# Graph layer with a sorted scatter: the load order at the start, the seam between two stages, and the pace of the sort's steps

## The chip, the cores and the metric

The kernel runs on one core of a Trainium2 chip. The time is device microseconds from start to end of one execution. PE is TensorE (matmuls; PEld its weight loads), DVE is VectorE, ACT is ScalarE, POOL is GpSimd and SP is SyncE, which here only issues transfers. Each engine works through its own list of instructions in order.

## The reference

```python
def reference(x, src, dst, edge_weight, L0_gnn_weight, L0_ffn_W, L0_ffn_b):
    # x (8192, 512); src, dst, edge_weight (131072,)
    h = layernorm(x) @ L0_gnn_weight.T
    x = x + segment_sum(edge_weight[:, None] * h[dst], src, 8192)
    x = x + ffn(layernorm(x))
    return x
```

`ffn` takes a few columns of a normalized row, turns groups of 16 into two small numbers, sends them through seven layers of width 160, and adds one-hot codes of the two rounded results to 32 columns, where a mask holds. It returns the normalized rows with these codes added. The edges come in the order of `dst`, while the sum runs over `src`: the kernel sorts them itself by blocks of 128 values of `src`.

## The kernel before

The nodes are 64 blocks of 128 rows. The edges of a block are cut into tiles of 128: 6 tiles a block in a first part (384 tiles) and 11 in a second (704). For a tile, POOL gathers 128 rows of h from HBM with an indirect DMA (`rows_for`, L546), DVE makes a matrix with the edge's weight in the column of its row (`hot_for`, L559, a "one-hot", seven buffers of four tiles ahead), and PE multiplies the two and sums over the block's tiles (`blocks_of`, L841, two matmul passes a tile). Each buffer of four tiles also has one small matmul (L837). Six buffers of gathered rows exist (pool `gp`), so gathers can run at most 24 tiles ahead.

The work is in three stages, whose instructions are written out by hand in one order for PE, DVE, ACT and SP (`manual_schedule`).

1. **h** (`project`, L469 to L525). For 64 blocks: load x in pairs (L476, SP), statistics on DVE (`scale`, L484 to L488), normalization on ACT (L490), transposition by PE (`turn`, L499) and a copy by ACT (L501), the product by PE (L518), a copy by ACT (L520), the store to `h_rows` (L524, L522, SP). Between the blocks, the sort of the first part is dealt out.
2. **The first part's 384 tiles** (`begin`, L845). Sums are added to x (L851) and stored. Between the tiles, the sort of the second part is dealt out.
3. **The second part's 704 tiles** (`evenly`, L872). The sums give the final x; `ffn` works on units of eight blocks between the tiles.

The sort (`order`, L456) is a generator of steps. It has chunks of edges, 7 in the first part and 9 in the second (`chunk`, L248): DVE compares blocks (L254), PE sums over rows (L262), DVE sums over columns (L267) and masks (L271), PE makes ranks (L277), DVE makes places (L281 to L304, with casts by ACT, L295), and 512 matmul passes in groups put edges into their places (L321, after L313). Then `squeeze` (L329) closes the gaps: a scan (L338), and for ten bits a shift by masks on DVE (L394, L401, L408) with a copy on ACT (L398); at the end PE transposes the result (L446) and ACT writes the three arrays that say which row to gather, which row to add to, and with which weight (L448).

Each step ends with `yield tiles, blocks`: how many tiles of the first part (in stage 2), or blocks of h (in stage 1), are to pass before the next step. In stage 1 the loop adds up the second number in `due`; in stage 2 the first:

```python
            while t >= due:
                due += next(second, (NB * FT,))[0]
            if t == late_at:
                for _ in second:
                    pass
```

`late_at` is tile 355; what is left of the second sort is issued there at once, since the gathers of the second part need its result. In the first part a step works on whole rows (`fine` is 0), in the second on pieces of about 520 columns with one step each.

At the start, SP issues the loads of src, dst and the weights (L226 to L228) ahead of x (L476), ACT issues the load of the layer's weights (L156), and DVE prepares the edges (L233 to L241) ahead of the first statistics of x. After the last block of h, ten copies on ACT spread the weights of `ffn` (`spread_weights`, L213).

Of the kernel before, what the change touches and what calls it, by code (L numbers as in the profile page):

```python
# [13 lines left out]
OP = mybir.AluOpType  # L14
# [20 lines left out]
def tile_gnn_ffn(  # L35
# [51 lines left out]
    SHARE, WIDTH = 0.5, 640  # L87
# [68 lines left out]
    nc.scalar.dma_start(gw, gnn_wT.rearrange("(k p) e -> p k e", p=P))  # L156
# [12 lines left out]
    def rstd_of(pool, var_ap, n, name):  # L169
        r = pool.tile([P, n], F32, name=name)  # L170
        nc.scalar.activation(r, var_ap, AF.Sqrt, bias=eps)  # L171
        nc.vector.reciprocal(r, r)
        return r

# [45 lines left out]

    with tc.tile_pool(name="ld", bufs=1) as ld:
# [10 lines left out]

        nc.vector.tensor_scalar(low, src_i, 7, None, op0=OP.logical_shift_right)  # L233
        nc.vector.tensor_copy(blk, by_chunk(low))

# [12 lines left out]
    def chunk(ck, ps_c, q, col, fine):  # L248
# [3 lines left out]
        for cs in cut(GC, 2, fine):  # L252
            n = cs.stop - cs.start
            nc.vector.tensor_tensor(  # L254
                hot[:, cs], each.rearrange("p (o b) g -> p o b g", o=1).to_broadcast([P, n, NB, GQ]),
                blk[:, q, cs].rearrange("p c (o g) -> p c o g", o=1).to_broadcast([P, n, NB, GQ]),
                OP.is_equal)
            yield 1, 1 - fine
# [14 lines left out]
        yield 0, 2  # L273
# [35 lines left out]
        yield from prepare(0)  # L309
        yield from prepare(SUB)  # L310
        p_c = ps_c.tile([P, GQ, 2, HALF], F32, name="p_c")
        yield 0, 2
# [16 lines left out]
    def squeeze(part, sq, ps_q, fine):  # L329
# [57 lines left out]
        for bit in range(LOW, LOW + BITS):  # L387
# [16 lines left out]
            yield 0, SHARE  # L404
# [6 lines left out]
            yield 0, SHARE  # L411
# [56 lines left out]

    def project():  # L469

        pairs, parts = {}, {}

        def load(b0):
            if b0 < NB:
                t = gp.tile([P, GS, D], F32, name="g")
                nc.sync.dma_start(t[:, 0:2], rows_of(x, b0, 2))  # L476
                pairs[b0] = t

        def scale(b0):
            t = pairs[b0]  # L480
            mv = mp.tile([P, 2, 2], F32, name="mv_h", bufs=2)
            for j in range(2):
                st = mp.tile([P, 6], F32, name="st_h", bufs=2)
                nc.vector.bn_stats(st, t[:, j])  # L484
                nc.vector.bn_aggr(mv[:, j, :], st)
            rstd = rstd_of(mp, mv[:, :, 1], 2, "rstd_h")
            nmr = mp.tile([P, 2], F32, name="nmr_h", bufs=2)
            nc.vector.scalar_tensor_tensor(nmr, mv[:, :, 0], -1.0, rstd, op0=OP.mult, op1=OP.mult)  # L488
            for j in range(2):
                nc.scalar.activation(t[:, 2 + j], t[:, j], AF.Identity, bias=nmr[:, j : j + 1],  # L490
                                     scale=rstd[:, j : j + 1])

        def turn(b):
            t = pairs[b - b % 2]
            if b % 2 == 0:
                parts[b] = gp.tile([P, GS, D], F32, name="g")
            p_t = ps_g.tile([P, D], F32, name="p_g")
            for k in range(KD):
                nc.tensor.transpose(p_t[:, k * P : (k + 1) * P],  # L499
                                    t[:, 2 + b % 2, k * P : (k + 1) * P], ident)  # L500
            nc.scalar.copy(parts[b - b % 2][:, b % 2], p_t)  # L501

        for b0 in (0, 2, 4):
            load(b0)
        for b0 in (0, 2):
            scale(b0)
        turn(0)
        for b in range(NB):
            if b % 2 == 0 and b + 4 < NB:
                scale(b + 4)  # L510
            if b + 1 < NB:
                turn(b + 1)
            if b % 2 == 1:
                load(b + 5)
            t = parts[b - b % 2]
            p_h = ps_g.tile([P, D], F32, name="p_g")
            for k in range(KD):
                nc.tensor.matmul(p_h, t[:, b % 2, k * P : (k + 1) * P], gw[:, k, :],  # L518
                                 start=(k == 0), stop=(k == KD - 1))
            nc.scalar.copy(t[:, 2 + b % 2], p_h)  # L520
            if b >= NB - 2:
                nc.sync.dma_start(rows_of(h_rows, b, 1), t[:, 2 + b % 2 : 3 + b % 2])  # L522
            elif b % 2:
                nc.sync.dma_start(rows_of(h_rows, b - 1, 2), t[:, 2:4])  # L524
            yield  # L525
# [36 lines left out]
    man_ctx = ExitStack()  # L562
    man_ctx.enter_context(tc.manual_schedule(engines={PE, DVE, ACT, SP}))
    first, second, heads = order(0), order(1), project()
# [6 lines left out]
    LEAD = 2  # L571
    due, early = LEAD, 0
    for b, _ in enumerate(heads):
        while first and due <= b + 1:
# [3 lines left out]
            else:  # L578
                due += step[1]
        if first is None:  # L580
# [5 lines left out]
    assert first is None  # L586
    for t in range(early, AHEAD * GS):
        hot_for(t)
    spread_weights()
# [255 lines left out]
    def begin():  # L845
# [11 lines left out]
        for b, k, p_g in blocks_of(0):  # L857
# [5 lines left out]
            if k == TILES[0] - 1:  # L863
                last = (b, p_g)
            while t >= due:
# [250 lines left out]
```

## Time and profile before

| | |
|---|---|
| median of 13 runs | 2143.88 us (2127.63 to 2154.27) |
| the profiled execution | 2144.66 us; span of its instructions 2142.7 us |
| granted TensorE clock, mean | 0.903 |
| PE busy | 1763.1 us, 82% |
| DVE busy | 990.9 us, 46% |
| ACT busy | 388.5 us, 18% |
| POOL busy | 1123.0 us, 52%, of it gathers 1100.0 (1088 of 1011 ns) |
| DMA | 391.37 MB, 183 GB/s |
| chain that ended last | PE 61%, another queue 14%, DVE 13%, "issue" 7% |

The span is what lies between the first and the last instruction. The page of a profile gives busy time by engine, the span in 40 slices, the chain of work that ended last, and groups of instructions by line. A line of the timeline has the start in us, the duration, the engine, the line of the kernel, the operation, the tile written and those read, the shape, and how many instructions were put together; in brackets is the idle time of the engine before it, and what ended it. "issue" means that the profile shows nothing that the engine waited for. A table of stretches has one row for each stretch: its length, the busy time of each engine with a count, the granted clock, the share of time that the DMA engines were busy, and GB/s.

### The profile page before, as it was taken

The page shows a single profiled execution, that of the slowest core. Times are in us where ns is not written, and L with a number is a line of the kernel's source. Part 1 is how long each engine was busy: PE and PEld are TensorE (multiplying, and loading weights), DVE is VectorE, ACT ScalarE, POOL GpSimd, SP SyncE. Part 2 cuts the span into 40 slices and gives each one's busy share as a digit, 9 for nine tenths or more (in the row PEclk, how much of TensorE's full clock was granted, in tenths as well). Part 3 has the DMA queues.
Part 4 walks back from the last instruction along what each step waited for, and adds up shares of the span by engine and source line. Part 5 has one row for each costly group of instructions (what it writes and reads, how often), then busy time and mean ns, then how long its engine had stood idle before and what let it go on. Part 6 is the DMA issues. An engine that isn't in the chain of part 4 may idle for free.

```text
span 2142.7 us, 24058 instructions
## 1 busy us (share of the span) xinstructions
PE 1763.1 (82%) x9273; PEld 850.7 (40%) x9288; DVE 990.9 (46%) x2520; ACT 388.5 (18%) x520; POOL 1123.0 (52%) x1138
## 2 busy tenths in 40 slices
PE   6999977769889988893878598696978969787977
PEld 3655543334444444441322243342433324243444
DVE  5666577335555456489323235233342434234322
ACT  3555544301111111111000010100101001010111
POOL 4000000366666667668566666566666666656550
PEclk9999998879998999897899899797989979888986
DMA  4222322466676677676596657576676856757551
GB/s 149 91 88 88 110 79 79 143 210 208 202 239 206 188 232 216 195 222 197 181 308 179 189 166 262 167 247 196 177 258 180 265 173 207 227 163 242 182 151 42
DMA packets 140923, 391.37 MB, mean 183 GB/s; under 512 B 20352, under 2 KB 21376, under 8 KB 140800
## 3 DMA queue, kind: packets, MB, share of 16 engines
q0 software_dynamic: 87952, 286.45, 44.3%
q1 hardware_dynamic: 52320, 102.25, 14.0%
q8 instruction: 76, 1.25, 0.2%
q10 hardware_dynamic: 528, 1.05, 0.1%
q14 instruction: 47, 0.39, 0.1%
HBM read 339.33 MB, written 50.33 MB: 182 GB/s over the span
## 4 chain that ended last, share of the span: by engine, by line
PE 61%; another core or an unknown queue 14%; DVE 13%; issue 7%; ACT 3%; POOL 2%; DMA 0%; ACTq 0%; DVEq 0%; POOLq 0%
PE p_g L841 33%; PE p_g L518 8%; PE p_c L321 7%; DVE hot L559 3%; PE p_a L637 2%; PE p_a L639 2%; POOL g L546 2%; ACT blocks L295 1%; PE p_rank L277 1%; DVE w L408 1%; PE p_base L262 1%; PE p_g L499 1%; DVE word L408 1%; DVE word L401 1%
## 5 line engine op out<-in xcount | busy, mean ns | idle before, releaser
L546 POOL DMA_INDIRECT g<-h_rows,at_dst x1088 | 1100.0, 1011 | 954.3 <-issue 686.4
L841 PE MATMUL p_g<-g,hot 128*128 128x512 f32 x2176 | 1102.4, 641 | 39.6 <-issue 38.0
L841 PEld LDWEIGHTS p_g<-g,hot 128*128 128x128 f32 x2176 | 407.4, 200 | 437.1 <-issue 426.5
L559 DVE TENSOR_SCALAR hot<-lanes,at_row,at_w 128x128 f32<-128x128 f32 x1088 | 325.9, 355 | 183.7 <-remote 95.7
L518 PE MATMUL p_g<-xg,g 128*128 128x512 f32 x512 | 241.9, 617 | 32.3 <-ACT g L501 32.3
L321 PE MATMUL p_c<-put,blocks 128*64 128x40 f32 x4096 | 164.3, 240 | 57.8 <-issue 47.0
L321 PEld LDWEIGHTS p_c<-put,blocks 128*64 128x64 f32 x4096 | 148.8, 149 | 105.2 <-issue 103.7
L295 ACT CAST blocks<-hot 128x1024 f32<-128x1024 bf16 x64 | 130.7, 2081 | 307.7 <-issue 238.6
L518 PEld LDWEIGHTS p_g<-xg,g 128*128 128x128 f32 x512 | 95.9, 197 | 135.6 <-issue 98.2
L611 DVE TENSOR_SCALAR hb<-p_b,b_b 128x128 f32<-128x128 f32 (+1 forms) x54 | 18.1, 335 | 224.2 <-PE p_b L631 124.3
L304 DVE TENSOR_TENSOR put<-at,val_a 128x640 f32<-128x640 bf16 x64 | 52.7, 824 | 131.9 <-remote 100.0
L837 PEld LDWEIGHTS <-hot 128*1 128x1 bf16 x272 | 21.6, 79 | 228.4 <-issue 201.1
L267 DVE TENSOR_TENSOR cum<-cum,hot 128x512 bf16<-128x512 bf16 x112 | 47.6, 425 | 111.4 <-issue 66.1
L892 DVE TENSOR_TENSOR xu<-xu,p_g 128x512 f32<-128x512 f32 x64 | 43.7, 682 | 94.8 <-remote 64.5
L837 PE MATMUL p_j<-g,hot 128*1 128x4 bf16 x272 | 45.7, 168 | 45.6 <-DMA g<-h_rows,at_dst 28.5
L171 ACT ACTIVATE rstd_f<-mv_f,eps 128x8 f32<-128x8 f32 (+1 forms) x9 | 2.7, 301 | 438.7 <-issue 185.4
L614 ACT ACTIVATE ha<-p_a,b_a 128x512 f32<-128x512 f32 (+1 forms) x54 | 34.6, 640 | 235.0 <-PE p_a L639 95.9
L851 DVE TENSOR_TENSOR xg<-xg,p_g 128x512 f32<-128x512 f32 x64 | 43.6, 681 | 65.8 <-PE p_g L841 45.0
L731 ACT COPY back<-p_v 128x256 f32<-128x256 f32 (+1 forms) x9 | 3.3, 371 | 344.4 <-PE p_v L729 258.2
L639 PEld LDWEIGHTS p_a<-hb,w_z 128*128 128x128 f32 x360 | 52.8, 211 | 19.0 <-issue 17.9
L725 DVE COPY v<-p_v 128x128 f32<-128x128 f32 (+1 forms) x9 | 2.5, 277 | 120.9 <-remote 120.2
L729 PE MATMUL p_v<-ident,pick 128*128 128x128 f32 (+1 forms) x18 | 5.8, 422 | 63.7 <-DVE v L725 63.7
(179 smaller groups left out, 1241.6 us busy)
## 6 DMA issues: line engine op xcount, KB each, us to landing
g<-h_rows,at_dst POOLq DMA_INDIRECT x1088
g<-in_x_dram SPq DMA_DIRECT2D x32, 512.0 KB
xg<-in_x_dram SPq DMA_DIRECT2D x16, 1024.0 KB
x_rows<-xg SPq DMA_DIRECT2D x32, 512.0 KB
xu<-x_rows SPq DMA_DIRECT2D x16, 1024.0 KB
h_rows<-g SPq DMA_DIRECT2D x31, 512.0 KB
out_dram<-xu SPq DMA_DIRECT2D x7, 2048.0 KB
xg<-in_gnn_wT_dram ACTq DMA_DIRECT2D x1, 1024.0 KB
```

The source lines that it names most:

```text
L267: nc.vector.tensor_tensor(cum[:, c], cum[:, c - 1], hot[:, c - 1], OP.add)
L295: nc.scalar.copy(blocks, hot[:, c0 : c0 + SUB].rearrange("p c b g -> p c g b"))
L304: nc.vector.tensor_tensor(put[:, :, :, i, :], at[:, cs], v.to_broadcast([P, n, 2, HALF]), OP.mult)
L321: nc.tensor.matmul(p_c[h * NB : (h + 1) * NB, g], blocks[:, c, g, :], put[:, k, h], start=False, stop=last)
L518: nc.tensor.matmul(p_h, t[:, b % 2, k * P : (k + 1) * P], gw[:, k, :], start=(k == 0), stop=(k == KD - 1))
L546: nc.gpsimd.indirect_dma_start(out=g[:, k, :], out_offset=None, in_=h_rows, in_offset=bass.IndirectOffsetOnAxis(ap=at_dst[part][:, i : i + ...
L559: nc.vector.tensor_scalar(hots[n][:, k, :], lanes, at_row[part][:, i : i + 1], at_w[part][:, i : i + 1], op0=OP.is_equal, op1=OP.mult)
L639: nc.tensor.matmul(p_a[:, g, :], w_z[:, i, g, :], last_hb, start=False, stop=((g + 1) * T % 512 == 0 or g == NG - 1))
L837: nc.tensor.matmul(p_j[:, part, :], hot[:, GS - 1, :].bitcast(BF16)[:, 1:2], g.rearrange("p k d -> p (k d)").bitcast(BF16).rearrange("p (k ...
L841: nc.tensor.matmul(p_g, hot[:, i, :], g[:, i, :], start=(k == 0), stop=(k == TILES[part] - 1))
L851: nc.vector.tensor_add(xg[:, b % G, :], xg[:, b % G, :], p_g)
L892: nc.vector.tensor_add(xj, xj, p_g)
```

## The change

Five things are changed.

- At the start, ACT loads its function table, then issues the load of x's first pair, then that of the layer's weights. `project` becomes a generator whose first steps are dealt among the edge operations: the statistics of the first pair stand ahead of all edge operations, its scaling and transposition behind the first two of them, the rest behind.
- Paces in blocks of h: within a chunk two blocks before the ranks become 1.5; two before the places become one before and one after the second `prepare`; each half of a bit takes 0.7 blocks (`TURN`), not 0.5. In the second part the first comparison no longer counts 0 for all four pieces: the last counts 1.
- After the first part's sort has ended, up to 25 steps of the second part's first chunk (`BEGUN`) are dealt among the last blocks of h; all steps up to the 41st are issued behind the last block, ahead of the first tile.
- Paces in tiles: a step of a chunk still takes 1.0 tiles, one of `squeeze` 0.85 (`PACE`).
- `spread_weights` moves from behind h to tile 96 of stage 2.

Lines are numbered anew in the changed kernel: L262 becomes L342, L277 L357, L321 L402, L353 L434, L446 L527, L499 L213, L501 L215, L518 L238, L520 L240, L546 L570, L559 L583, L837 L866, L841 L870, L851 L880.

```diff
-    SHARE, WIDTH = 0.5, 640
+    SHARE, TURN, WIDTH, PACE = 0.5, 0.7, 640, (1.0, 0.85)
...
-    nc.scalar.dma_start(gw, gnn_wT.rearrange("(k p) e -> p k e", p=P))
...
+        load(0, nc.scalar)
+        nc.scalar.dma_start(gw, gnn_wT.rearrange("(k p) e -> p k e", p=P))
+        yield
+        mv, rstd = weigh(0)
+        yield
+        scale(0, mv, rstd)
+        turn(0)
+        yield
+        load(2)
+        load(4)
+        scale(2, *weigh(2))
...
+    nc.scalar.activation(over[:, 0:1], eps, AF.Sqrt)
+    heads = project()
+    next(heads)
...
+        next(heads)
         nc.vector.tensor_scalar(low, src_i, 7, None, op0=OP.logical_shift_right)
         nc.vector.tensor_copy(blk, by_chunk(low))
+        next(heads)
...
-            yield 1, 1 - fine
+            yield 1, cs.stop // GC
...
-        yield 0, 2
+        yield 0, 1.5
...
         yield from prepare(0)
+        yield 0, 1
         yield from prepare(SUB)
...
-        yield 0, 2
+        yield 0, 1
...
-            yield 0, SHARE
+            yield 0, TURN
...
-            yield 0, SHARE
+            yield 0, TURN
...
-                yield from chunk(ck, ps_c, q, col, fine)
+                for tiles, blocks in chunk(ck, ps_c, q, col, fine):
+                    yield tiles * PACE[0], blocks
...
-            yield from squeeze(part, sq, ps_q, fine)
+            for tiles, blocks in squeeze(part, sq, ps_q, fine):
+                yield tiles * PACE[1], blocks
...
-    LEAD = 2
-    due, early = LEAD, 0
+    LEAD, BEGUN = 2, 25
+    due, early, begun = LEAD, 0, 0
...
+        while first is None and begun < BEGUN and due <= b + 1:
+            due += next(second)[1]
+            begun += 1
...
+    for n in range(BEGUN + 16):
+        if n >= begun:
+            next(second)
...
-    spread_weights()
...
+            if t == NBUF[0]:
+                spread_weights()
             while t >= due:
```

`weigh` is the first half of the old `scale` (statistics and square root), `scale` the second.

More of the change, by code (lines that the diff above doesn't have):

```diff
@@ L173, in rstd_of, with project, load, weigh @@
         return r
+    def project():
+        pairs, parts = {}, {}
+        def load(b0, engine=nc.sync):
+            if b0 < NB:
+                t = gp.tile([P, GS, D], F32, name="g")
+                engine.dma_start(t[:, 0:2], rows_of(x, b0, 2))
+                pairs[b0] = t
+        def weigh(b0):
+            t = pairs[b0]
+            mv = mp.tile([P, 2, 2], F32, name="mv_h", bufs=2)
+            for j in range(2):
+                st = mp.tile([P, 6], F32, name="st_h", bufs=2)
+                nc.vector.bn_stats(st, t[:, j])
+                nc.vector.bn_aggr(mv[:, j, :], st)
+            rstd = mp.tile([P, 2], F32, name="rstd_h", bufs=2)
+            nc.scalar.activation(rstd, mv[:, :, 1], AF.Sqrt, bias=eps)
+            return mv, rstd
+        def scale(b0, mv, rstd):
+            t = pairs[b0]
+            nc.vector.reciprocal(rstd, rstd)
+            nmr = mp.tile([P, 2], F32, name="nmr_h", bufs=2)
+            nc.vector.scalar_tensor_tensor(nmr, mv[:, :, 0], -1.0, rstd, op0=OP.mult, op1=OP.mult)
+            for j in range(2):
+                nc.scalar.activation(t[:, 2 + j], t[:, j], AF.Identity, bias=nmr[:, j : j + 1],
+                                     scale=rstd[:, j : j + 1])
+        def turn(b):
+            t = pairs[b - b % 2]
+            if b % 2 == 0:
+                parts[b] = gp.tile([P, GS, D], F32, name="g")
+            p_t = ps_g.tile([P, D], F32, name="p_g")
+            for k in range(KD):
+                nc.tensor.transpose(p_t[:, k * P : (k + 1) * P],
+                                    t[:, 2 + b % 2, k * P : (k + 1) * P], ident)
+            nc.scalar.copy(parts[b - b % 2][:, b % 2], p_t)
+        load(0, nc.scalar)
[9 more added lines that the diff above has]
+        scale(2, *weigh(2))
+        for b in range(NB):
+            if b % 2 == 0 and b + 4 < NB:
+                scale(b + 4, *weigh(b + 4))
+            if b + 1 < NB:
+                turn(b + 1)
+            if b % 2 == 1:
+                load(b + 5)
+            t = parts[b - b % 2]
+            p_h = ps_g.tile([P, D], F32, name="p_g")
+            for k in range(KD):
+                nc.tensor.matmul(p_h, t[:, b % 2, k * P : (k + 1) * P], gw[:, k, :],
+                                 start=(k == 0), stop=(k == KD - 1))
+            nc.scalar.copy(t[:, 2 + b % 2], p_h)
+            if b >= NB - 2:
+                nc.sync.dma_start(rows_of(h_rows, b, 1), t[:, 2 + b % 2 : 3 + b % 2])
+            elif b % 2:
+                nc.sync.dma_start(rows_of(h_rows, b - 1, 2), t[:, 2:4])
+            yield
@@ L219, in spread_weights @@
             nc.scalar.copy(w_z[GB * g : GB * g + 3, 0, g, :], w_in[GB * g : GB * g + 3, 0, 0:P])
+    man_ctx = ExitStack()
+    man_ctx.enter_context(tc.manual_schedule(engines={PE, DVE, ACT, SP}))
+    nc.scalar.activation(over[:, 0:1], eps, AF.Sqrt)
+    heads = project()
+    next(heads)
     with tc.tile_pool(name="ld", bufs=1) as ld:
@@ L465, in order @@
                 tc.tile_pool(name="ps_q", bufs=2, space=PSUM) as ps_q:
-            yield from squeeze(part, sq, ps_q, fine)
[L469 to L525, printed above, removed]
@@ L560, in hot_for @@
                                 at_w[part][:, i : i + 1], op0=OP.is_equal, op1=OP.mult)
-    man_ctx = ExitStack()
-    man_ctx.enter_context(tc.manual_schedule(engines={PE, DVE, ACT, SP}))
-    first, second, heads = order(0), order(1), project()
+    first, second = order(0), order(1)
     def load_x(b0):
```

## The prediction

> **What bounds the kernel now.** I first read the page's 40 slices and then the table of stages (busy time of each engine per stretch), because the three stages have different limits. The stage of h, up to 401 us, is TensorE's. In the first part's blocks (412 to about 1057 us) TensorE shares with the sort of the second part. In the second part's blocks the gathers set the pace. Two places stand out. The first is a stop around 1000 us:
>
> ```profile
> 980.00:1000.00 20.00, 9.81 (x20) 3.62 (x18) 19.89 (x37) 4.50 (x3) 16.65 (x12) 0.89 0.64 204
> 1000.00:1020.00 20.00, 0.00 (x0) 0.00 (x0) 19.79 (x32) 4.14 (x4) 15.73 (x15) 0.50 0.63 182
> 1040.00:1060.00 20.00, 20.00 (x49) 8.15 (x48) 6.14 (x18) 0.00 (x0) 15.20 (x16) 1.00 0.76 235
> ```
>
> The columns are the stretch, then PE, PEld, DVE, ACT and POOL busy with counts, the granted clock, and DMA. PE is at 0 while DVE is full. The timeline of PE names the releaser:
>
> ```profile
> 990.11 3.70 PE L841 MATMUL p_g<-g,hot 128*128 128x512 f32 x8
> 1023.56 1.54 PE L446 MATMUL p_f<-ident,dst_f 128*128 128x128 f32 x6 [29.75 <-DVE dst_f L431]
> ```
>
> Counting L841's pairs in that timeline, 356 of the first part's 384 tiles are done there: at tile 355 (`late_at`) all sort steps that are left are issued at once, with TensorE's transposes of the result (L446) ahead of tile 356. So PE waits for DVE to drain the sort. The second place is the seam between h and the gathers:
>
> ```profile
> 404.82 1.01 POOL L546 DMA_INDIRECT g<-h_rows,at_dst  x1 [378.46 <-issue]
> 412.52 0.17 PE L837 MATMUL p_j<-g,hot 128*1 128x4 bf16 x1 [11.48 <-DMA g<-h_rows,at_dst]
> 412.62 6.69 PE L841 MATMUL p_g<-g,hot 128*128 128x512 f32 x8
> ```
>
> PE is idle 11.5 us for the first gathered rows, and the first eight matmuls then take 6.69 us where later rows have 3.70.
>
> The price of a gather comes next, from the busy time of L546 alone in stretches of the trace (stretch, POOL busy, clock, DMA):
>
> ```profile
> 945.00:967.00 22.00, 18.06 (x13) 1.00 0.81 250
> 967.00:990.00 23.00, 19.32 (x13) 0.85 0.78 241
> 1156.00:1180.00 24.00, 18.20 (x20) 0.93 0.67 194
> ```
>
> Undisturbed, one is issued every 1.25 us (1.2 here, with the two at the edges). While DVE is full with the bits of the sort it is every 1.73 us (45 us for 26). A tile's two matmuls take 0.93 us, so wherever the sort's bits run, the gathers are the limit.
>
> **The change, part by part.** I follow the start of the gather with number 380 (from 0), at 1034.83 us in the profiled execution, the first after the stop. From there on 708 gathers remain in either kernel, and I move that whole rest with it. Stages and steps are counted in the programs' instruction order.
>
> *Start.* Before, DVE's seven edge operations (L233 to L241, 5.45 to 13.2 us) stand ahead of x's first statistics at 13.19, and the first transposes are at 17.94. Now x's first pair is loaded on ACT's queue, behind the table load (1.28 us) that is moved there, and ahead of the 1 MB of gnn_wT; SP still issues the edges first. If x lands at 7 to 9 us (the edges' first 512 KB took 4.7 us from issue to landing), the first transposes come at about 13. But the transposed block 1 is copied by ACT behind the scaling of pairs 2 and 4, whose statistics stand behind five edge operations (4.9 us). Chaining: 12 + 4.9, statistics 1.7, square root and two small steps 0.7, the same again for pair 4 overlapped, scaling 1.5, copy 0.6: block 1's matmuls start at 24 to 25 instead of 27.69. I take **-3 us** (0 to -5).
>
> *Chunks of the first part.* 5.5 blocks of h instead of 6. PE's work is unchanged (a block 3.87 us, a chunk 11.4: 1.73 for L262, 1.73 for L277, 7.7 for L321, 0.23 for L313), so a chunk's 36.8 us hold 34.6 of work and 2.2 of waits on L501. In three of seven chunks one block, not two, now lies between L262 and L277; the chain between them is a copy 0.59, seven adds 3.19 and a product 2.29, with handovers 6.5 us, against 3.87: +2.6 each. On the other side the two casts of L295 (4.05 us in one go on ACT, behind which L501 waits) are now a block apart, which may return up to 7. **0** (-7 to +8).
>
> *1.4 blocks a bit.* In the present squeeze DVE is full and PE waits every second block:
>
> ```profile
> 309.96 5.12 PE L518 MATMUL p_g<-xg,g 128*128 128x512 f32 x8 [4.59 <-ACT g L501]
> ```
>
> L353 to L446 take 75 us over 11 blocks (42.6 us of PE). The new order has 16 blocks there (41 to 57). DVE's own sort work is 57 us; eight pairs of blocks add 2.34 us each of statistics; waits for the copies of w (L398) about 7: 83 us in all, against 75 + 5 x 3.87 = 94. **-11** (-6 to -16). DVE is the limit either way, so more blocks would not help.
>
> *Second part's first chunk.* 25 steps now stand in blocks 58 to 63: L262, L277, L313 and a quarter of L321 add 5.6 us of PE, and L277 is again one block behind L262, +2.7. **+8**. The end of h so moves by -6, to 395. The other 16 steps stand behind the last block: three quarters of L321 (5.8 us at the first part's 7.7 a chunk) and one L262 (1.73). With the casts between, their chain is some 8 us and fits in the 11.5 us hole, as h's last copies are ahead of them on ACT and nothing is added to SP. If the hole did not cover them they would cost 8; a warm clock at 412.62 would give 3 back. **0** (-3 to +8). The weight copies (L213, 4 us of ACT at 401) move to tile 96, where no DVE step needs ACT for longer than its slack: 0.
>
> *One chunk less beside the gathers.* Each costs 33 tiles there, and far more than its PE work:
>
> ```profile
> 544.79 1.89 PE L262 MATMUL p_base<-hot,above 128*128 128x512 bf16 x7
> 597.05 1.89 PE L262 MATMUL p_base<-hot,above 128*128 128x512 bf16 x7
> ```
>
> Eight such distances from 491.4 to 930.9 average 54.9 us (1.66 a tile), since L321 has "issue" gaps there that it has not in h. The first distance is 71.1, with a stretch at 438 to 453 us in which single matmuls come every 1.4 us. Now L353 of the second part stands at tile 261 instead of 302. From 406.5: 30 tiles, 50 us at the steady pace or 66 as before; I take 58; then 7 x 54.9. L353 comes at 849 us (930.9 before).
>
> The Trainium skill (Runtime: NRT & Kernel Launch, Instruction fetch mechanics) says that loading instructions is mostly hidden. If the gaps are such loads, the trace disagrees; by the page the 30 tiles would take 50 us and the forecast would be 8 lower.
>
> *Squeeze and stop.* Pace 0.85 spreads the steps over tiles 261 to 353, with the transposes at 353: nothing is left for `late_at`. Before, L353 to gather 380 took 103.9 us for 58 gathers (322 were issued). Now 281 are issued when it starts (a lead of 20, as now), 99 are to come. DVE's 99 us from 924.9 to 1024 hold some 80 of sort; with 92 one-hots at 0.255 and 15 adds at 0.6 it needs 112 us. In that time the lead is used up, and 72 gathers are needed. At 1.73 they take 125 us; at the 1.42 that the trace shows at 927.8 to 942, where DVE was three quarters busy, 102. DVE would be about 94% busy, so I take 1.65: 119 us. Then 27 at 1.25: 34. Gather 380 starts at 849 + 153 = 1002, **-33**. The stop's 38 us do not simply vanish: most of them come back as gathers slowed by the sort.
>
> A rule speaks against this spreading. The Trainium skill (SBUF — State Buffer, "A bandwidth-pool intuition that's wrong") says that descriptors of POOL's DMAs are blocked while a VectorE operation holds the shared ports: 0.62 us becomes 3.1. Adding 2.5 to each of the 72 gathers would give +151 us on my 119. The rows show 1.73, not 3.7, with one-hots between the sort's steps, and I follow the rows.
>
> *After it*: PE starts the second part with less lead, which costs gathers nothing: 0 (-10 to +5). **Sum**: -33 on the 2144.66 us of the profiled execution (span 2142.7), which is 0.8 over the median of the 13 runs: **2112 us**.
>
> **Rivals.**
> 1. The seam is clean and gathers keep 1.45 in the squeeze: -8 for the first 30 tiles, 72 x 0.2 = -14: 2090. For it: PE starved means DVE has gaps. Against: 1.73 in the only stretch with bits.
> 2. The change gives the stop up but takes its place elsewhere: h not shorter (+11), the seam sticks out (+8), gathers at 1.75 (+7): 2138. For it: L321 beside gathers is slow from the first microsecond.
> 3. It does not do what it says, the sort outlasting tile 355 again: DVE would need over 1.35 us a tile; a rest of 15 us would stop PE: 2127. The order of steps speaks against it.
> 4. Slower: DVE's steps lock out the gathers. Where six steps followed each other with no one-hot between, at 987.70, one gather took 4.86 us. At pace 0.85 pairs of steps follow each other. If the mean over the 72 is 2.4 us, that is +54: 2166. It decides from (119 + 33) / 72 = 2.1 us on.
>
> **Numbers.** Forecast 0.62, rival 1 0.18, rival 2 0.10, rival 3 0.04, slower 0.06. Range 2085 to 2137: the bounds above, -27 to +25, with rival 1 and most of rivals 2 and 3. This kernel's runs tell about 0.3% (6.4 us) from no change: faster 0.87, same 0.07, slower 0.06.
>
> **What would show it.** PE's last h matmul near 395; L837's first wait under 5 us, with L321 ahead of it; the second part's squeeze line (L353 before) near 849; L546 every 1.6 to 1.7 us for 120 us after it; no PE gap over 10 us at the transposes (L446 before); gather 380 near 1002. I am wrong if gathers in the squeeze need 2 us, if the first 30 tiles take 70, or if the second part's blocks take longer than now.

## The result and the profile after

The changed kernel takes 2191.94 us (median of 10 runs, 2184.74 to 2199.99), the kernel before 2143.81 (46 runs): ratio **1.0228, interval 1.0205 to 1.0251**. It is slower by 48 us, where 2112 us, 32 less than before, were forecast. Its profiled execution has a span of 2186.3 us (2142.7 before) and a granted clock of 0.900.

First the stage of h. Block starts and ends of PE's products (L518 before, L238 after), read from the two timelines:

| stretch | before, us | after, us | difference | forecast |
|---|---|---|---|---|
| start of block 9 | 74.0 | 67.9 | -6.1 | -3 |
| blocks 9 to 41 (chunks of the first part) | 194.4 | 250.8 | **+56.4** | **0** |
| blocks 41 to 57 (bits of the squeeze) | 106.2 | 83.1 | -23.1 | -11 |
| block 57 to the end of h | 26.4 | 37.8 | +11.4 | +8 |
| end of h | 401.0 | 439.6 | +38.6 | -6 |

The stretches fit the steps of the forecast only roughly: with shorter chunks the squeeze begins three to four blocks earlier, so that more of the sort lies ahead of block 41 and less behind it. What each step did by itself is told further below.

The groups by line of both pages (busy time, mean ns of one | idle before, and what ended it) show what PE waits for. Before:

```profile
L518 PE MATMUL p_g<-xg,g 128*128 128x512 f32 x512 | 241.9, 617 | 32.3 <-ACT g L501 32.3
```

and after:

```profile
L238 PE MATMUL p_g<-xg,g 128*128 128x512 f32 x512 | 255.1, 645 | 43.5 <-ACT g L215 43.5
L357 PE MATMUL p_rank<-cum,eye 128*128 128x512 bf16 x128 | 31.7, 392 | 38.7 <-DVE cum L351 38.7
```

These sums hide the matter: before, only 7.9 of the 32.3 us lie in the chunks (74 to 269 us), after 29.6 of the 43.5 (60 to 320 us). The timeline of PE in one chunk of the changed kernel, with the waits in brackets:

```profile
105.73 1.89 PE L342 MATMUL p_base<-hot,above 128*128 128x512 bf16 x7
...
118.19 6.13 PE L238 MATMUL p_g<-xg,g 128*128 128x512 f32 x8 [6.27 <-ACT g L215]
...
133.97 6.77 PE L238 MATMUL p_g<-xg,g 128*128 128x512 f32 x8 [3.60 <-ACT g L215]
...
156.48 1.89 PE L342 MATMUL p_base<-hot,above 128*128 128x512 bf16 x7
```

This chunk takes 50.8 us; a chunk of the kernel before took 36.8. Two waits of 6.3 and 3.6 us are seen, and the eight matmuls behind each take 6.1 and 6.8 us instead of 3.6. The table of stretches has the granted clock for it (in the column ahead of the DMA share), for this chunk of six blocks and the next one, of five, and then for the two slow groups of eight alone:

```profile
105.70:156.50 50.80, 40.87 (x346) 22.73 (x346) 23.27 (x41) 20.64 (x28) 0.00 (x0) 0.87 0.19 63
156.50:192.30 35.80, 31.37 (x334) 18.64 (x334) 23.29 (x41) 19.41 (x26) 0.00 (x0) 1.00 0.27 89
118.20:124.30 6.10, 6.10 (x9) 2.56 (x10) 0.00 (x0) 0.91 (x2) 0.00 (x0) 0.60 0.00 0
134.00:140.70 6.70, 6.70 (x9) 2.63 (x9) 0.96 (x2) 2.80 (x3) 0.00 (x0) 0.54 0.00 0
```

So a wait of PE is paid twice: once as such, once by the clock behind it, 0.60 and 0.54 against 1.00. Together the two waits (9.9 us) and the slow matmuls (5.7 us) cost 15.6 us; a chunk of before has some 1.5 us of waits, and the difference is the 14 us by which this chunk is longer.

Of the seven chunks, two begin at an odd block and have six blocks (13 to 18 and 35 to 40): they take 50.8 and 51.2 us. The two of six blocks that begin at an even one take 35.9 and 35.8. The three of five blocks take 39.9, 35.8 and 39.0, where 36.8 less one block's 3.87 would be 33. All seven take 288 us for 39 blocks; in the kernel before they took 258 us for 42.

Then the seam. The lines that answer to those of before:

```profile
443.45 1.01 POOL L570 DMA_INDIRECT g<-h_rows,at_dst  x1 [417.80 <-DVE put L384]
451.23 0.17 PE L866 MATMUL p_j<-g,hot 128*1 128x4 bf16 x1 [1.25 <-issue]
451.33 3.70 PE L870 MATMUL p_g<-g,hot 128*128 128x512 f32 x8
485.49 3.29 PE L357 MATMUL p_rank<-cum,eye 128*128 128x512 bf16 x8 [26.17 <-DVE cum L351]
```

The forced steps (those issued at once behind the last block) fill the hole, the first tile starts 11.7 us behind the end of h (11.6 before) and its matmuls are at full speed. But behind the seventh tile PE stands for 26 us. The timeline of ACT shows where: the copy of the sums, which PE had finished at 450.0, starts at 476.9. ("remote" stands for an event whose sender the profile doesn't hold.)

```profile
462.14 0.29 ACT L407 COPY cells_a<-p_c 128x160 f32<-128x160 f32 x1 [18.32 <-issue]
462.33 0.30 ACT L407 COPY cells_w<-p_c 128x160 f32<-128x160 f32 x1
476.89 0.58 ACT L344 CAST cum<-p_base 128x512 bf16<-128x512 f32 x1 [14.27 <-remote]
```

The gathers alone, by stretches (POOL busy, clock, DMA), in the squeeze and behind it:

```profile
930.00:955.00 25.00, 18.38 (x14) 0.96 0.68 212
980.00:1005.00 25.00, 20.43 (x16) 0.91 0.75 230
1200.00:1225.00 25.00, 16.01 (x17) 0.83 0.58 169
```

They take 1.66 us each from number 281 to 353 (forecast 1.65). The stop at the transposes is still there, though nothing is forced at tile 355 any more. PE's timeline:

```profile
1050.25 0.82 PE L527 MATMUL p_f<-ident,dst_f 128*128 128x128 f32 x6
...
1070.09 1.11 PE L527 MATMUL p_f<-ident,w_c 128*128 128x128 f32 x4 [11.25 <-issue]
```

and the stretch it falls in:

```profile
1060.00:1080.00 20.00, 6.79 (x14) 3.15 (x15) 2.57 (x8) 2.22 (x8) 9.60 (x12) 0.53 0.49 142
```

Unlike before, DVE isn't full here (2.57 us of 20): PE and ACT hand each other the result in steps of 3 to 11 us. Gather 380 starts at 1083.7 us, 48.9 later than before. The rest of the kernel is 5.3 us shorter, so the spans differ by 43.6.

### The profile page after: what moved, and what is told of

It reads as the page before. It is cut to its first block, busy times and chain, and to the rows that moved or that the text cites. A ratio compares the mean times of both kernels' runs of the same rounds, so it can differ in the third digit from the quotient of the medians.

```text
span 2186.3 us, 24076 instructions
## 1 busy us (share of the span) xinstructions
PE 1765.4 (81%) x9273; PEld 849.5 (39%) x9288; DVE 987.1 (45%) x2520; ACT 389.5 (18%) x521; POOL 1111.3 (51%) x1138
## 3 DMA queue, kind: packets, MB, share of 16 engines
q8 instruction: 76, 1.25, 0.2%
## 4 chain that ended last, share of the span: by engine, by line
PE 54%; another core or an unknown queue 16%; DVE 12%; issue 9%; POOL 4%; ACT 2%; DMA 2%; ACTq 0%; DVEq 0%; POOLq 0%
PE p_g L870 29%; PE p_g L238 8%; PE p_c L402 6%; POOL g L570 4%; DVE hot L583 3%; PE p_a L668 2%; PE p_a L666 2%; DMA g<-h_rows,at_dst 1%; PE p_rank L357 1%; PE p_base L342 1%; DVE cum L347 1%; DVE cum L351 1%; DVE st_h L192 1%; DVE ln L706 1%
## 5 line engine op out<-in xcount | busy, mean ns | idle before, releaser
L570 POOL DMA_INDIRECT g<-h_rows,at_dst x1088 | 1089.1, 1001 | 1009.5 <-DVE put L384 417.8
L870 PE MATMUL p_g<-g,hot 128*128 128x512 f32 x2176 | 1097.0, 641 | 20.3 <-issue 18.6
L870 PEld LDWEIGHTS p_g<-g,hot 128*128 128x128 f32 x2176 | 408.6, 201 | 415.7 <-issue 404.7
L583 DVE TENSOR_SCALAR hot<-lanes,at_row,at_w 128x128 f32<-128x128 f32 x1088 | 324.8, 353 | 192.8 <-remote 114.9
L238 PE MATMUL p_g<-xg,g 128*128 128x512 f32 x512 | 255.1, 645 | 43.5 <-ACT g L215 43.5
L402 PE MATMUL p_c<-put,blocks 128*64 128x40 f32 x4096 | 157.8, 234 | 50.0 <-issue 46.4
L402 PEld LDWEIGHTS p_c<-put,blocks 128*64 128x64 f32 x4096 | 142.5, 143 | 93.5 <-issue 89.1
L238 PEld LDWEIGHTS p_g<-xg,g 128*128 128x128 f32 x512 | 101.0, 208 | 153.5 <-issue 105.7
L866 PEld LDWEIGHTS <-hot 128*1 128x1 bf16 x272 | 21.5, 79 | 257.1 <-issue 219.2
L347 DVE TENSOR_TENSOR cum<-cum,hot 128x512 bf16<-128x512 bf16 x112 | 47.8, 427 | 121.6 <-ACT cum L344 100.5
L866 PE MATMUL p_j<-g,hot 128*1 128x4 bf16 x272 | 45.7, 168 | 68.8 <-DMA g<-h_rows,at_dst 37.4
L880 DVE TENSOR_TENSOR xg<-xg,p_g 128x512 f32<-128x512 f32 x64 | 43.7, 683 | 47.0 <-PE p_g L870 41.9
L357 PE MATMUL p_rank<-cum,eye 128*128 128x512 bf16 x128 | 31.7, 392 | 38.7 <-DVE cum L351 38.7
L240 ACT COPY g<-p_g 128x512 f32<-128x512 f32 x64 | 37.3, 583 | 96.4 <-PE p_g L238 96.4
```

The lines of the kernel that those rows point to most:

```text
L347: nc.vector.tensor_tensor(cum[:, c], cum[:, c - 1], hot[:, c - 1], OP.add)
L357: nc.tensor.matmul(p_rank, eye, cum[:, :, i * nb : (i + 1) * nb, :], start=(i == 0), stop=(i == GC - 1))
L402: nc.tensor.matmul(p_c[h * NB : (h + 1) * NB, g], blocks[:, c, g, :], put[:, k, h], start=False, stop=last)
L570: nc.gpsimd.indirect_dma_start(out=g[:, k, :], out_offset=None, in_=h_rows, in_offset=bass.IndirectOffsetOnAxis(ap=at_dst[part][:, i : i + ...
L583: nc.vector.tensor_scalar(hots[n][:, k, :], lanes, at_row[part][:, i : i + 1], at_w[part][:, i : i + 1], op0=OP.is_equal, op1=OP.mult)
L866: nc.tensor.matmul(p_j[:, part, :], hot[:, GS - 1, :].bitcast(BF16)[:, 1:2], g.rearrange("p k d -> p (k d)").bitcast(BF16).rearrange("p (k ...
```

## The experiments

One plain fact is needed for the numbers. The experiments ran in five groups, each with the kernel before in it. In three of them that kernel took 2121 to 2145 us and the profiles have a mean clock of 0.90 to 0.92, as in the first result; in two it took 1897 and 1900 us, with clocks of 0.94 to 0.96. All comparisons are ratios to the kernel before in the same group, and I call the two kinds of group 2130 and 1900. The expectations speak of kinds of chips. That is not shown: the record has chip 10 for two groups of the 2130 kind and chip 3 for one of the 1900 kind, but chip 11 for one of each.

| run | kind | ratio to before | interval | h ends | first tile | gather 380 |
|---|---|---|---|---|---|---|
| changed kernel | 2130 | 1.0228 | 1.0205 to 1.0251 | 439.6 | 451.3 | 1083.7 |
| changed kernel again | 1900 | 1.0164 | 1.0133 to 1.0195 | 440.0 | 451.7 | 984.3 |
| 6 blocks a chunk | 2130 | 0.9977 | 0.9957 to 0.9996 | 382.1 | 426.6 | 1008.0 |
| 6 blocks, split kept | 2130 | 0.9991 | 0.9969 to 1.0014 | 376.3 | 422.3 | 1023.1 |
| 6 blocks, begun a block later | 1900 | 1.0396 | 1.0373 to 1.0418 | 476.9 | 504.2 | 1023.2 |
| the same, pairs' work later too | 2130 | 0.9961 | 0.9931 to 0.9992 | 378.0 | 426.8 | 1011.8 |
| before, with 5.5 blocks only | 1900 | 1.0209 | 1.0182 to 1.0236 | 438.4 | 450.1 | 986.5 |
| before, with the new start only | 1900 | 0.9988 | 0.9974 to 1.0003 | 397.6 | 409.4 | 949.5 |

### The chunks in h

The theory: a chunk of 5.5 blocks falls out of step with the pairs of blocks in which x's statistics are made. The first two runs take the changed kernel and give a chunk six blocks again.

```diff
-        yield 0, 1.5
+        yield 0, 2
         p_rank = ps_c.tile([P, GC, NB // GC, GQ], F32, name="p_rank")
...
         yield from prepare(0)
-        yield 0, 1
         yield from prepare(SUB)
...
-        yield 0, 1
+        yield 0, 2
```

> Changed kernel with the old paces inside a chunk of h (two blocks before the ranks, two before the places in one piece): 6 blocks a chunk, in step with the pairs of blocks. Theory 1 (a chunk of 5.5 blocks falls out of step with the pairs, and DVE's statistics then stand behind the chunk's chain): blocks 9 to 41 take about 36.8 us a chunk again, h ends near 395 (439.6 in the changed kernel), total about 2192 - 45 = 2147. Rival (the start, or the clock by itself, slows the chunks): h ends within 10 us of 440, total within 10 us of 2192. The steps left over at the end of h are more here, so the seam may stick out by 5 to 10 us.

> Changed kernel with two blocks before the ranks, but the two before the places still split in one and one: 6 blocks a chunk, the casts a block apart. Theory 1 (parity decides): as good as the unsplit form, h ends at 390 to 400. Rival (the split itself puts DVE's products ahead of the statistics): h ends above 415, and the unsplit form is at least 20 us faster.

For the second run only the first pair of lines is changed. They end h at 382.1 and 376.3 us instead of 439.6, 57 and 63 us earlier, and blocks 9 to 41 take 194.7 and 189.6 us, against 194.4 in the kernel before: the whole loss of the chunks is gone. (A few us of the earlier end come from fewer steps of the second part in h.) The split of the places costs nothing. Both rivals fall.

Whether the number of blocks or the phase decides is told by this six-block form with every chunk begun one block later:

```diff
-    LEAD, BEGUN = 2, 25
+    LEAD, BEGUN = 3, 25
```

> The form with 6 blocks a chunk, but the first part's sort begun one block later (the first step falls due at block 3 instead of 2). Every chunk keeps its 6 blocks, and all of them now begin at an odd block, between the two blocks of a pair; nothing else is changed. In the changed kernel the two chunks that began at odd blocks and had 6 blocks (13 to 19, and from 35) took 50.8 and 51 us, those that began at even blocks 35.8. Theory 1 (the phase of a chunk against the pairs of blocks decides): all seven chunks take about 50, h ends about 14 x 7 = 98 us later than the 382 to 384 of the form with 6 blocks, near 480; total +4 to +5% over it. Rival (5.5 blocks are too few for the work of a chunk, whatever the phase): h ends one block later at most, within 10 us of 384, total the same.

h ends at 476.9, as expected (near 480), and the kernel is 4% slower than before, with the instructions of the six-block form and the same six blocks. Here is one of the seven equal chunks. PE:

```profile
89.99 0.60 PE L213 MATMUL p_g<-ident,g 128*128 128x128 f32 x4
96.92 5.49 PE L238 MATMUL p_g<-xg,g 128*128 128x512 f32 x8 [6.33 <-ACT g L215]
...
114.37 5.29 PE L238 MATMUL p_g<-xg,g 128*128 128x512 f32 x8 [5.93 <-ACT g L215]
```

DVE in the same time:

```profile
86.93 3.18 DVE L347 TENSOR_TENSOR cum<-cum,hot 128x512 bf16<-128x512 bf16 x7 [7.61 <-ACT cum L344]
90.15 2.29 DVE L351 TENSOR_TENSOR cum<-cum,hot 128x4096 bf16<-128x4096 bf16 x1
92.36 0.68 DVE L192 BATCH_NORM_STATS2 st_h<-g 128x6 f32<-128x512 f32 x1
```

and ACT:

```profile
94.15 0.30 ACT L195 ACTIVATE rstd_h<-mv_h,eps 128x2 f32<-128x2 f32 x1 [7.25 <-DVE mv_h L193]
94.88 1.52 ACT L204 ACTIVATE g<-g,nmr_h,rstd_h 128x512 f32<-128x512 f32 x2 [0.43 <-DVE nmr_h L202]
96.30 0.56 ACT L215 COPY g<-p_g 128x512 f32<-128x512 f32 x1
```

Read upwards from PE. The product at 96.92 waits for the copy of its transposed block (L215). The transposition was done at 90.6, but on ACT the copy stands behind the scaling of the next pair (L204), that behind its square root (L195), and this waits for the pair's statistics (L192). On DVE these stand behind the adds and the product of the chunk (L347, L351), which could begin only when PE's sums (L342) had been copied. PE, ACT and DVE thus go round once in a row while nothing else is ready for PE. In a chunk that begins at an even block, an odd block without any pair's work lies between L342 and the statistics; the statistics come a block later against PE's demand, and the waits are 0.7 us. The six-block form in step (here the run without forced steps, told of below), in the same part of a chunk:

```profile
112.04 3.60 PE L238 MATMUL p_g<-xg,g 128*128 128x512 f32 x8
115.48 1.89 PE L357 MATMUL p_rank<-cum,eye 128*128 128x512 bf16 x8
117.20 0.60 PE L213 MATMUL p_g<-ident,g 128*128 128x128 f32 x4
118.53 3.70 PE L238 MATMUL p_g<-xg,g 128*128 128x512 f32 x8 [0.73 <-ACT g L215]
```

If that is the way, moving the pairs' statistics and scaling by one block as well must heal the late phase:

```diff
-            if b % 2 == 0 and b + 4 < NB:
-                scale(b + 4, *weigh(b + 4))
+            if b % 2 == 1 and b + 3 < NB:
+                scale(b + 3, *weigh(b + 3))
```

> The form whose chunks all begin one block later (h ended at 476.9 there), with x's statistics and scaling for a pair also moved by one block: they now stand ahead of odd blocks instead of even ones. The chunks keep their phase against the count of blocks, and the pairs' work is moved by as much. Theory 1 in its exact form (TensorE waits because the statistics and the scaling of a pair stand on VectorE and ScalarE straight behind a chunk's chain, ahead of the next block's copy): the two waits of 6 us a chunk go, h ends at 382 to 390, total as the form with 6 blocks, ratio 0.985 to 0.995. Rival (a chunk's phase costs by itself, through its own casts or ranks): h still ends above 440, ratio above 1.02.

h ends at 378.0, and the waits of 6 us in the chunks are gone (0.7 us again). The phase of the chunk costs nothing by itself; it is the order of the pair's work and the chunk's chain on DVE and ACT. This settles the cause.

Last, the step alone, in the kernel before (the three lines of the first diff, the other way):

> The kernel before with nothing but the paces inside a chunk changed (1.5 blocks before the ranks, one before and one behind the second part of the places). The forecast gave this 0 (-7 to +8) with the cost in h alone. Theory 1: blocks 9 to 41 take some 50 us longer, h ends at 440 to 455 instead of 401, total +40 to +55 us or +2 to +2.8%. Rival (the chunks are slow only together with the new start or with 1.4 blocks a bit): total within 8 us of the kernel before.

Blocks 9 to 41 take 250.6 us (194.4 before), +56. Of this, 17 us come back in blocks 41 to 57 (89.0 us, 106.2 before), where less of the sort is left, and h ends at 438.4, 37 us later than before. The total is +39.6 us (1.0209 of 1897), at the lower edge of the expectation. This one step, forecast at 0, accounts for the whole loss in this group, where all changes together give 1.0164. And the start alone (six blocks, 1.0 blocks a bit, no steps of the second part in h, pace 1.0, weights' copies behind h):

> The changed start alone: 6 blocks a chunk, 1.0 blocks a bit, no step of the second part in h, pace 1.0, the weights' copies behind h. The forecast gave it -3, the trace of the changed kernel shows -5 to -7 in blocks 0 to 9; nothing behind it should differ from the kernel before: total -3 to -7 (ratio 0.997 to 0.9985). If the new order of the start were at fault for the slow chunks (rival to the theory of parity), h would end 40 us later.

The ratio, 0.9988 (0.9974 to 1.0003), is -2.3 us on 1900, not clear of no change; h ends 3.4 us earlier than before, and as much is already there at block 9 (70.6 against 74.0). The start is not at fault.

### The waits at the seam and at the transposes

My first theory was that ACT waits for its next instructions. Padding it with 36 more tiny instructions at the start should move the place:

```diff
-    nc.scalar.activation(over[:, 0:1], eps, AF.Sqrt)
+    for _ in range(37):
+        nc.scalar.activation(over[:, 0:1], eps, AF.Sqrt)
```

> Changed kernel with 36 more tiny ScalarE instructions at the start, where ScalarE waits for x; nothing else is changed. In the changed kernel ScalarE stands still 18 and 14 us behind its 390th instruction (443.8 to 476.9 us) and again 22 and 11 us behind its 517th (1032 to 1069), each time just past a multiple of 128, with an 8 KB instruction load on record at 446.4 and 1041.2. Theory 2 (ScalarE waits for its next instructions while gathers run): the wait of 26 us ahead of the first ranks after the seam goes, as the 390th instruction now falls into h, and the one at the transposes moves to an earlier place; total -15 to -50, 2145 to 2175. Rival (the place itself, such as the gathers' beginning, makes ScalarE slow): both waits stay where they are, total within 6 us of 2192.

Both waits stayed at their places: ratio 1.0200 (1.0166 to 1.0235). The one at the transposes is as long as before (23.4 us); the one ahead of the ranks (L358 here, at 483) has 13.9 instead of 26.2 us, and why it is shorter stays open. The padding itself made h end 9.7 us later. Moving the weights' copies alone, which takes instructions away ahead of the seam, did nothing either:

> Kernel before, with only the copies of the ffn weights moved from behind h to tile 96. This takes about 14 instructions away ahead of the seam on ScalarE, so that its 390th is no longer in the idle hole at 405 to 422 us but at the boundary of two chunks, near 487. Theory 2: a wait of 15 to 30 us on ScalarE appears there, total +5 to +25 (2149 to 2169). Rival (and the forecast's price): nothing but 4 us of idle ScalarE time moves, total within 3 us of 2144.

1.0006 (0.9978 to 1.0034). The theory, by which the first wait had to go, the second to move and a new one to appear here, falls. It leaves the forecast's price of 0 for these copies right.

The form with six blocks showed the next theory. There all 24 gathers of the first buffers run from 386 to 418 us while the forced steps are under way, and PE's short sums (L401 here, L402 in the changed kernel) come in ones to sixes with gaps that end in "issue", until shortly after the last of these gathers. Holding the first gather until the steps are through tests it; the copy leaves the numbers as they are:

```diff
     for n in range(BEGUN + 16):
         if n >= begun:
             next(second)
+    nc.scalar.copy(at_dst[0][:, 0:1], at_dst[0][:, 0:1])
```

> The form with 6 blocks a chunk, and one more tiny copy on ScalarE behind the steps that are issued behind h: it rewrites the first column of the row numbers, so the first gather has to wait until these steps are through. Without it the first gather starts at 385.9, TensorE's sums of the chunk then come in fours with gaps from 396.7 to 419.6 us, run at full speed again 2 us after the 24th gather, and the first tile starts at 426.5. Theory 3 (gathers issued back to back slow the short matmuls and the handovers of the other engines): the chunk's sums take 8 us in one go, the first gather starts at 400 to 405, the first tile at 408 to 413, 14 to 18 us earlier; total -5 to -15 against the form without the copy. Rival (the slow sums are TensorE's own, with no tie to the gathers): the first tile moves to about 434 or later, total +5 to +10.

> The changed kernel with the same tiny copy ahead of the first gather. There ScalarE stood from 443.8 to 476.9 us though TensorE was through with its sums at 448 and 450, while 24 gathers were issued back to back from 443.5 to 473.5. Theory 3: ScalarE's copies follow TensorE at once (within 1 us), the wait of 26 us ahead of the first ranks falls below 8, tile 8 starts near 470 instead of 489.7; total -10 to -20 (2172 to 2182). Rival: the wait stays and everything moves by the 6 us that the gathers start later, total +6.

> The changed kernel once more, beside the others. The chips that gave the first traces and the one that gave the last differ: there the chunk's sums beside gathers had gaps with nothing to wait for, here they have none, and the whole kernel takes 1900 instead of 2144 us. Theory 3, narrowed (what slows the other engines beside gathers belongs to the chip or the moment, not to the kernel): on a chip with a clock near 0.96 the wait of 26 us ahead of the first ranks and the 24 us at the transposes are gone, h still ends near 440, ratio to the kernel before 1.015 to 1.02; on a chip with a clock near 0.90 both are there again, ratio 1.02 to 1.025. Rival (they belong to the kernel's order): both waits on any chip.

These three met groups of the 1900 kind, where nothing is slow beside gathers even without a hold: the changed kernel has neither the 26 us nor the 24 us there (ahead of tile 7 and at the transposes PE waits for less than 1 us at a time). The groups of L402 show the same for its sums, first in the changed kernel of the first result,

```profile
L402 PE MATMUL p_c<-put,blocks 128*64 128x40 f32 x4096 | 157.8, 234 | 50.0 <-issue 46.4
```

and in the 1900 group:

```profile
L402 PE MATMUL p_c<-put,blocks 128*64 128x40 f32 x4096 | 131.6, 231 | 0.4 <-ACT blocks L375 0.4
```

So they tell only that the order of the kernel alone doesn't make the waits; the held forms gave 0.9931 (0.9902 to 0.9959) and 1.0168 (1.0139 to 1.0198). Side by side in a group of the 2130 kind the hold could be judged:

> The form with 6 blocks a chunk and forced steps, once more, beside the next one. On a chip where the kernel before takes about 2120 its chunk's sums behind h took 29 us (391 to 420) beside the first gathers and the first tile started at 426; if this chip is such a one, the same again. On a chip where it takes 1900: no gaps, first tile within 4 us of 405.

> The same with the first gather held until the forced steps are through. Theory 3 (gathers slow the other engines where the chip shows such gaps): on a chip near 2120 the sums take 8 us, the first tile starts at 408 to 413, 14 to 18 us ahead of the form without the hold, total -5 to -15 against it. On a chip near 1900, where nothing is slow: first tile up to 6 us later than without the hold, total 0 to +6. Rival: the gaps are there with the hold as well, first tile at 430 or later on the slow chip.

PE without the hold, first gather at 384.8:

```profile
393.29 0.34 PE L401 MATMUL p_c<-put,blocks 128*64 128x40 f32 x5 [0.29 <-issue]
...
416.78 0.23 PE L401 MATMUL p_c<-put,blocks 128*64 128x40 f32 x1 [1.17 <-issue]
417.49 0.33 PE L401 MATMUL p_c<-put,blocks 128*64 128x40 f32 x1 [0.48 <-issue]
418.88 6.05 PE L401 MATMUL p_c<-put,blocks 128*64 128x40 f32 x129 [1.07 <-issue]
```

and with it:

```profile
392.13 5.48 PE L401 MATMUL p_c<-put,blocks 128*64 128x40 f32 x128 [3.45 <-DVE put L384]
397.88 4.08 PE L401 MATMUL p_c<-put,blocks 128*64 128x40 f32 x128 [0.27 <-ACT blocks L375]
```

The same sums take 35 us beside the gathers and 10 without; the first tile starts at 408.3 instead of 426.8. The theory holds for these sums, in this kind of group; how gathers slow them is not shown. Slow loads of PE's instructions, a rival to it, don't fit: the traces have two instruction loads of 16 KB beside these sums in either form, of 1.2 and 1.4 us without the hold and 1.0 and 1.3 us with it; without it there is none between 396 and 421 us, where most of the gaps lie. That ACT's 26 us at the seam of the changed kernel have the same cause was not tested in a 2130 group. The gain doesn't last: at tile 30 the two forms stand at 479.8 and 480.4: the next chunk's sums lie beside gathers in both, and the held form pays there. The ratios, 0.9951 (0.9920 to 0.9982) and 0.9924 (0.9892 to 0.9956), can't be told apart.

### Versions without forced steps

```diff
-    for n in range(BEGUN + 16):
-        if n >= begun:
-            next(second)
```

with six blocks a chunk; then 0.95 for 1.0 tiles a step; then once more in a group of the other kind, beside the form with both shifts.

> The form with 6 blocks a chunk without the steps that are forced behind h: what is left of the second part's first chunk is dealt among the tiles. Theory 3: the first tile starts near 395 (8 to 11 us behind the first gather) instead of 426, but the chunk's sums now stand between tiles and are slow there; tile 63 at 515 to 535 (538 with the forced steps), total -5 to -20 against that form. Rival (the forced steps only move a cost): tile 63 within 5 us of 538, total the same within 5 us.

> The form with 6 blocks a chunk and no steps forced behind h, with 0.95 instead of 1.0 tiles a step in the second part's chunks. With 1.0 the sort still lasted past tile 355 and TensorE stood 16.8 us at the transposes. 9 chunks of 33 steps, less those in h, end 14 tiles earlier, so the transposes fall due at about tile 353 with nothing left to force. Expected: the 16.8 us fall below 5, the 380th gather starts 0 to 12 us earlier, total 0 to -12 against the 0.9867 of the form before. Rival: the gathers in the squeeze are slower by as much, no gain.

> The form with 6 blocks a chunk and no steps forced behind h, beside the next one. On a chip near 1900 it gave 0.987. On a chip near 2120 the sums that are taken out of the seam stand between tiles beside gathers, where the chunk's sums are slow as well (in the held form they cost back by tile 30 all that the seam had gained): ratio 0.988 to 0.997 there, tile 30 between 465 and 482.

> The same with the sort begun a block later and the pairs' statistics and scaling a block later too. With forced steps this pair of shifts ended h at 378.0 instead of 380.9. Expected: h ends 2 to 6 us earlier than in the form beside it, total 0 to -6 against it, within the interval of 0.3%; rival: without forced steps the later begin leaves a step more to the tiles, no gain at all.

| run | kind | ratio | interval | first tile | tile 63 | gather 380 |
|---|---|---|---|---|---|---|
| 6 blocks, nothing forced | 1900 | 0.9867 | 0.9841 to 0.9893 | 396.1 | 485.0 | 930.8 |
| the same, 0.95 a step | 1900 | 0.9884 | 0.9858 to 0.9910 | 393.5 | 482.9 | 929.1 |
| 6 blocks, nothing forced | 2130 | 0.9933 | 0.9890 to 0.9977 | 394.0 | 520.9 | 1030.5 |
| the same, both shifts | 2130 | 0.9908 | 0.9874 to 0.9942 | 389.7 | 509.0 | 1004.9 |

All are faster than both kernels, than the one before by about 1%. Against the six-block form with forced steps a gain is shown only in a 1900 group, and there against the one with the hold (0.9867 and 0.9931, intervals apart); in the 2130 groups the intervals overlap (0.9933, against 0.9977 and 0.9951). The pace of 0.95 brings the gap of 16.8 us at the transposes down to 3.3 and gains nothing: gather 380 starts only 1.7 us earlier, and the rival given with it is right. The form with both shifts ends h 4.6 us earlier than the one beside it, as expected, but their totals overlap.

## Why the prediction was wrong

The step that failed is **"Chunks of the first part"**: 0 (-7 to +8). Alone it made h end 37 us later (+56 in blocks 9 to 41, -17 behind them), and blocks 9 to 41 of the changed kernel lost the same 56 us. I chained what a shorter chunk does to itself (PE's ranks behind DVE's adds: "+2.6 each", and these waits of about 2.4 us at L357 are there) and to ACT's casts. I did not chain what it does to the other stream on the same in-order engines: the statistics of x, made in pairs. The kernel before hid this, because six blocks are three pairs and every chunk had the same good phase. I had seen waits of 2.2 us a chunk on L501, the same releaser, and took them for a constant. Neither the range nor the slower rival covered it; the rival I gave for slower, gathers at 2.1 us in the squeeze, did not occur (1.66).

The steps, in the profiled executions; where nothing else is said, of the changed kernel in the first result:

| step | forecast | measured |
|---|---|---|
| start | -3 | -3.4 alone, at block 9 and at the end of h |
| chunks of the first part | 0 (-7 to +8) | +37 alone, at the end of h |
| 1.4 blocks a bit | -11 (-6 to -16) | -6 behind the shorter chunks (blocks 41 to 57: 89.0 with the old pace, 83.1); -18 in the six-block form against the start alone |
| second part's first chunk | +8 | +11 |
| seam | 0 | 0.1, and 26 us behind the seventh tile |
| first 30 tiles | 58 | 78.9 |
| seven chunks beside gathers | 7 x 54.9 = 384 | 397 |
| squeeze to gather 380 | 153 | 156.6 |
| the rest | 0 | -5.3 |

- *Start* and *1.4 blocks*: right in mechanism. Block 1's product starts at 22.5 us, where 24 to 25 were forecast. The slower pace of the bits brings 6 us behind short chunks and 18 behind long ones. The -23 in blocks 41 to 57 is mostly the shift of the sort, not the pace: 17 us of it appear with shorter chunks alone.
- *Seam*: right at the seam itself. The wait behind it, with 79 instead of 58 us for 30 tiles, is what was named as ground for being wrong ("if the first 30 tiles take 70"). It was not there in the 1900 group, where these tiles take 45.3 us. The 66 us "as before" in the forecast are not what the kernel before shows for them: its first 30 tiles take 59.7 us (412.5 to 472.2).
- *Squeeze*: right in its first term, 72 gathers at 1.65 (1.66 measured); the 27 behind them took 41 us, not 34, with the stop at the transposes among them. By the rule of the Trainium skill (SBUF — State Buffer, "A bandwidth-pool intuition that's wrong") that I had weighed against it, a DMA of POOL that takes 0.62 us alone takes 3.1 beside a copy on VectorE. A delay of that size on every gather doesn't show here: 1.66 us from one to the next, with DVE busy 106.5 of 120 us.
- *Stop at the transposes*: forecast gone. In the 1900 group it is (waits below 0.5 us at L527 there); in the first result it came back as 24 us of slow handing over, in place of 30 us behind a full DVE.
- *One chunk less beside the gathers*: the largest gain of the sum. From the end of h to gather 380 it was to bring 27 us, with the seam and the new squeeze in it. In the first result this stretch cost 10 more (633.8 before, 644.1 after), and in the 1900 groups it brought 8 against the form with the new start alone (551.9 and 544.3 us). Where the sums are not slow, a chunk beside gathers costs 46 us and not 54.9 (tiles 30 to 261 of both runs, by seven), and moving it away is worth less.

On the sum of 33: 44.6 us of the miss lie in h (37 of them the chunks, 5 the bits that brought less behind them, 3 the second part's first chunk), 20.9 in the first 30 tiles, 12.6 in the next seven chunks, 3.6 in the squeeze, 0.2 in the seam, and 5.3 were given back behind it: 76.6 in all, the distance from -33 to the +43.6 of the spans. The chunks' part has its cause shown; what delays ACT in the first 30 tiles stays open.

## What to carry to other kernels

When the pace of one stream of work is changed against another, list for each in-order engine what stands behind what, over a whole period of both. A period that was a multiple of the other stream's (6 blocks, pairs) is a hidden assumption; 5.5 or a start one block later broke it, and it cost more than all planned gains together (37 us at the end of h, against 33). Test such a dependence by shifting one stream by a step, and then both: it takes two lines and tells phase from load.

## What the runs showed of the hardware

- The same program differs by 12% or more between groups of runs: 2121 to 2145 and 1897 to 1900 us for the kernel before. The stage of h is the same in both kinds to within 3 us (440.0 and 439.6 for the changed kernel). The difference begins with the gathers, although their own pace of issue, 1.25 us in the median, is the same.
- In the slower kind, while gathers are issued back to back, short matmuls come in small groups about 0.7 us or a multiple of it apart, and ACT starts up to 27 us after PE has finished what it waits for. In the other kind the same instructions run without such gaps. What makes the difference stays open. That holding the gathers removes the gaps of the sums behind h was shown (35 and 10 us), and that padding ACT with 36 instructions moves neither of its long waits. The traces of the slower kind record no landing of a gather, those of the other kind do for 136 to 544 of the 1088, so what ended a wait is read less surely in the slower kind.
- In h, behind a wait of PE of 3.5 to 6.3 us the next eight matmuls took 5.1 to 6.8 us instead of 3.6, in all 50 cases of the traces; behind waits of 1.9 to 3.4 us they took 3.7 in some and 5.4 to 6.5 in others. The granted clock was 0.60 and 0.54 in the two slow groups shown above, and 1.00 in the chunk of five blocks behind them.
